# A two-stage codebook convolution on one core: the head of the program reordered

## The chip, the cores and the metric

The kernel runs on one core of one Trainium2 chip. The metric is the device time of one execution in microseconds (us), the median of several runs. Before the change it is 2680.17 us (three runs, 2678.79 to 2683.46). All times in this document are in us unless ns stands there.

The core has five instruction streams that run side by side and wait for each other by semaphores: PE (TensorE, matrix products; its weight loads are shown as PEld), DVE (VectorE), ACT (ScalarE), POOL (GpSimd) and SP (SyncE, which here only issues transfers). Transfers (DMA) are issued by SP and, for some, by POOL, and run on 16 DMA engines. Matrix products read from the on-chip memory SBUF and write into PSUM, which has eight banks.

## The reference, cut to what matters

For each of 16 images (256 channels, 28 x 28) the reference normalizes the channels in groups of 8, runs two "convolutions by codebook", and adds gates and residuals:

```python
def amm_conv3x3(x, centroids, w_sub, stride=1):
    patches = jax.lax.conv_general_dilated_patches(x, (3, 3), (stride, stride), 'SAME')
    p = patches.reshape(B, C, s, Ho * Wo).transpose(0, 3, 1, 2)
    d = jnp.sum(p * p, axis=-1)[..., None] - 2.0 * jnp.einsum('bncs,cks->bnck', p, centroids) + ...
    attn = jax.nn.softmax(-d, axis=-1)
    lut = jnp.einsum('cks,cso->cko', centroids, w_sub)
    out = jnp.einsum('bnck,cko->bno', attn, lut)
...
out = amm_conv3x3(x, centroids1, wsub1); out = relu(bn(out))
out = amm_conv3x3(out, centroids2, wsub2); out = se_layer(bn(out))
return x + relu(out + x)          # the x of the inner sum is the normalized one
```

For each channel and pixel the nine taps of the 3 x 3 patch are compared with 16 centroids, a softmax over the 16 gives weights, and the weighted centroids go through a 9 x 256 matrix per channel.

## The kernel before, in words

**Blocks.** The kernel works in fp32. An image is cut into four blocks: two halves of the channels (`hh`) times two halves of the rows (`t`, 14 rows, 392 pixels). 16 images and two layers make 128 blocks, numbered j; block j begins in step g = 2j, and its work is spread over some four steps. What block j does:

- `patches` (L363) loads two tiles `pt` of 64 channels each, `p` = 0 and 1, from the padded image in DRAM (`home1` in layer 1, `home2` in layer 2). Each tile takes six transfers: for each row dy of the 3 x 3 window one of 16 x 8 runs (L368, the taps of columns 0 and 1) and one of 8 x 8 runs (L372, column 2). A tap s of a channel lies in partition `tap_row(s)` of the channel's 16 (L60); partitions that hold no tap hold 1.0 from a clearing at the start, and one of them, `BIAS_ROW`, carries a bias. There are two `pt` buffers in all, so a tile can be loaded only when the logits that read it one block earlier are done.
- `logits` (L377), four calls `mm` = 0 to 3, two for each tile: 16 small products each into two double banks of PSUM (32 records of PE each, because an fp32 product takes two passes). `exps` (L392) on ACT turns them into exponentials.
- `num_b` (L442), "nb" on PE: the sums over the 16 centroids and the numerator of tap 8. `split_r` and `join_r` (L456, L460) put the sums into `r`; `split_q` and `join_q` (L466, L471) put tap 8 into `qo`. The splits are on ACT, the joins on DVE, and both pairs read the same bank.
- `recip_dve` (L475) inverts `r` on DVE, and `spread` (L484) copies it to the rows of each tap by shuffles.
- `num_a` (L429), "na" on PE, four calls: the numerators of taps 0 to 7, scaled by `scale_a` on DVE (L506) or, for one of them, by `copy_a` on ACT and `scale_q` on POOL (L497). The results, `q`, stay in SBUF.
- `product` (L514), "acc" on PE: the 128 x 128 products with the sub-weights. The four blocks of an image are combined in seven products instead of eight (a Strassen scheme), with differences of `q` made on POOL (`mix`, L523) and sums and differences of sub-weights (`combine`, L202). Their order is in `PRODUCTS` (L43): the first, A11, uses block 0's `q`; the second, S1, uses the difference of blocks 1 and 0.

**The order is written out by hand.** `at(step, sub, function, ...)` puts a call into a table, and the table is run through in order of (step, sub) (L1101). Each engine carries out its instructions in exactly this order, and so does SP's queue of transfers. PSUM is dealt out in the same way: four double banks, and a role (`ROLES`, L47) minus half the step, modulo 4, says which (L111); `small_bank` (L278) is the same for small products.

**The head of the program.** Before the table starts, block 0's way is cleared by hand: the first image is loaded by halves, its statistics (`gn_stats`, `gn_mean`, `gn_var`, L308 to L343: DVE, two small products on PE with `gmat`, four small operations on POOL) give mean and scale, `gn_apply` (L348) normalizes on ACT into the padded tile `xpads`, and `to_home1` (L357) writes it to DRAM in two shifted copies. `norm0` (L1078) bundles this for half an image. Around it stand memsets of the `pt` tiles (L1087, L1091 on DVE, L1092 on POOL), and `center_wd` (L1084) which centres the centroids: squares on DVE, a product "sqp" on PE (L288), additions and a mean on DVE. The centring of the second half of the channels is put behind block 0's first logits, at (0, 1.95).

The second image is prepared beside block 0 and 1 (L993 to L1001): `load_x` at (2, 1.65), `gn_stats` at (3, 1.9), `gn_mean` at (3, 2.1), `gn_var` at (4, 2.1), `gn_apply` and `to_home1` at (5, 1.9) and (5, 1.92). For later images the same calls stand in other places of the table and are not touched. Sub-weights of layer 1 are loaded by `load_w` (L189) at steps 1, 3 and 6 as 128 x 9 runs of 512 bytes each.

Of the kernel before, what the change touches and what calls it, by code (L numbers as in the profile page):

```python
# [17 lines left out]
P = 128  # L18
# [39 lines left out]


def tap_row(s):  # L60
    dy, dx = divmod(s, 3)
    return dy + (0, 8, 3)[dx]

# [10 lines left out]
def kernel(  # L74
# [28 lines left out]
    p_ring = ctx.enter_context(tc.tile_pool(name="p_ring", bufs=1, space=PSUM))  # L103

    gmat = const.tile([P, P], F32, name="gmat")
    make_block_diagonal(nc, gmat, 8)
# [12 lines left out]
    def bank(name, step=None, role=None):  # L119
        return banks(name, step, role)[:, 0, :]  # L120

    def after(u, n):
        return None if u["step"] is None else u["step"] + n

    def view(t, off, dims):
        return bass.AP(t.tensor, t.offset + off, [list(d) for d in dims])
# [62 lines left out]
    def load_w(l, n, eng=None):  # L189
        hh, o = SLOTS[n]  # L190
        t = wl[n]
        eng = eng or nc.sync
        if l == 0:
            eng.dma_start(t, ws1[:, NS * hh : NS * hh + NS, o * P : (o + 1) * P])
        else:
            eng.dma_start(t[:, 0:8, :], view(d_wa, hh * 8 * P * C + o * P, [[C, P], [P * C, 8], [1, P]]))
            eng.dma_start(t[:, 8, :], d_wb[hh * P : hh * P + P, o * P : (o + 1) * P])
# [49 lines left out]
    mhalf = const.tile([P, NB], F32, name="mhalf")  # L247
    one = const.tile([P, 1], F32, name="one")
    nc.gpsimd.memset(one, 1.0)
    nc.gpsimd.memset(mhalf, -0.5)  # L250
# [27 lines left out]
    def small_bank(name, step):  # L278
        return bank(name, step, step and ROLES["small"][step % 2])

# [82 lines left out]
    def patches(u, p, single=None):  # L363
        hm = (home1 if u["l"] == 0 else home2)[u["b"]]
        at0 = ((u["hh"] * P + 8 * 8 * p) * 2) * HROW + RT * u["t"] * PW
        pt = u["pt", p]
        for dy in range(3):
            nc.sync.dma_start(  # L368
                pt[dy::8, :, : PTW - 2],
                view(hm, at0 + dy * PW, [[HROW, 16], [16 * HROW, 8], [1, PTW - 2]]),  # L370
            )
            (single or nc.sync).dma_start(  # L372
                pt[3 + dy :: 16, :, : PTW - 2],
                view(hm, at0 + dy * PW + 2, [[2 * HROW, 8], [16 * HROW, 8], [1, PTW - 2]]),
            )

    def logits(u, mm):  # L377
        bs = []
        for i in range(4):
            if i % 2 == 0:  # L380
                bs.append(banks("lg", after(u, mm // 2), ROLES["lg", mm][i // 2]))
            bk = bs[-1][:, i % 2, :]
            for c in range(4):
                nc.tensor.matmul(  # L384
                    bk[32 * c : 32 * c + 32, :N].rearrange("p (r w) -> p r w", w=W),
                    lhsT=wts["wd", u["hh"]][32 * i : 32 * i + 32, mm, c, :],
                    rhs=u["pt", mm // 2][32 * i : 32 * i + 32, 4 * (mm % 2) + c, :].rearrange("p (r w) -> p r w", w=PW)[:, :, :W],
                    start=True, stop=True,
                )
        u["lg", mm] = bs  # L390
# [523 lines left out]
    for j, u in enumerate(blocks):  # L914
# [22 lines left out]
        at(g + 2, 1.25, recip_dve, u)  # L937
        at(g + 2, 1.3, split_q, u)
        at(g + 2, 1.35, join_q, u)
        for i, mm in enumerate(SLOT_MM):  # L940
# [10 lines left out]
    for l in range(2):  # L951
        for b in range(B):
# [3 lines left out]
            for c, w, r, ks in PRODUCTS:  # L956
                step = g + c - (c == 5 and n == 0)
                at(step, 2.0, product, (n, c), us[r], w, ks, step=step)
            for mm in (1, 2, 3, 4, 0):
# [4 lines left out]
            c11, c12, c21, c22 = (0, 0), (0, 1), (1, 0), (1, 1)  # L964
            at(g + 6 - (n == 0), 0.0, acc_copy, l, b, c11, (n, 5))
            at(g + 6, 2.02, acc_copy, l, b, None, (n, 6))
# [17 lines left out]
            if l == 0:  # L984
# [8 lines left out]
                if b + 1 < B:  # L993
                    at(*((g - 2, 2.6) if b else (2, 1.65)), load_x, b + 1)
                    for q in range(NB):
                        at(*((g, 0.3) if b else (3, 1.9)), gn_stats, b + 1, q)
                    at(g + 3 - 2 * (b > 0), 2.1, gn_mean, b + 1, step=g + 3 - 2 * (b > 0))
                    at(g + 4 - (b > 0), 2.1, gn_var, b + 1, step=g + 4 - (b > 0))
                    for q in range(NB):
                        at(g + 5 - (b > 0), 1.9, gn_apply, b + 1, q)  # L1000
                        at(g + 5 - (b > 0), 1.92, to_home1, b + 1, q)  # L1001
            else:
# [19 lines left out]

    at(1, 1.65, load_w, 0, "A11")
    at(3, 1.65, load_w, 0, "S3")
# [61 lines left out]

    nc.vector.memset(pts[0][:, :4], 1.0)  # L1087
    norm0(0)
    for i in range(2):
        to_home1(0, 0, i)  # L1090
    nc.vector.memset(pts[0][:, 4:], 1.0)  # L1091
    nc.gpsimd.memset(pts[1], 1.0)  # L1092
    center_wd(0)
    norm0(1)
    at(0, 1.95, center_wd, 1)
    at(-0.5, 0.7, to_home1, 0, 1)
# [87 lines left out]
def _lay_out(inputs):  # L1184
# [45 lines left out]
    arrays["in_cwb1"] = cwb.reshape(P, -1)  # L1230
    arrays["in_ws1"] = ws
    cent, wsub = f(_NAMES[0] + "2"), f(_NAMES[1] + "2")
# [29 lines left out]
```

## Time and profile before

| what | value |
|---|---|
| median of 3 runs | 2680.17 |
| the profiled execution's own time | 2684.49 |
| its span (first to last instruction) | 2683.0 |
| mean granted clock of PE | 0.993 |
| PE busy | 2613.8 (97%) |
| DVE, ACT, POOL busy | 1773.8, 1354.7, 1903.7 |
| bytes moved, mean rate | 374.39 MB, 140 GB/s |
| first logits of block 0 start | 26.19 |
| first logits of block 4 (second image) start | 103.33 |

The profile was taken in one execution by the hardware profiler. In its rows an operation stands with its line of the kernel, what it writes and reads (`lg<-pt,wd` is the logits from patches and centroids), the shape, and the number of instructions; in the order of time a row has the start, the length and, in brackets, how long the engine was idle before it and what ended that wait. "issue" means that the profile shows no wait. The starts of PE's matrix products are recorded, their ends are modelled. The granted clock is the share of full speed that PE's throttle let through. SPq rows are transfers as they are issued, not as they land. Lines of the profile are quoted in the parts below where they are used.

### The profile page before, as it was taken

The numbers are of one execution on the slowest core, as the hardware profiler recorded it, in microseconds if no ns is written. First come the engines' busy times: TensorE is split into PE (matmuls) and PEld (weight loads), VectorE is DVE, ScalarE is ACT, GpSimd is POOL, SyncE is SP. The second block draws the span as 40 slices with busy tenths as digits, with TensorE's granted clock in tenths as the row PEclk, the third lists the DMA queues.
The fourth block names the chain that finished last, engine by engine and source line by source line (L and its number), as shares of the span: only waits on it lengthen the run. The fifth ranks groups of instructions, "written<-read, shape, count | busy, mean of one in ns | idle before, by whom it ended". The sixth has DMA issues, their size and how long they took to land.

```text
span 2683.0 us, 85705 instructions
## 1 busy us (share of the span) xinstructions
PE 2613.8 (97%) x36984; PEld 1261.1 (47%) x36984; DVE 1773.8 (66%) x3786; ACT 1354.7 (50%) x1873; POOL 1903.7 (71%) x1334
## 2 busy tenths in 40 slices
PE   4999999999999999999999999999999999999997
PEld 1344444444444444444444444444444444444444
DVE  4785666667666556656577767677767677767675
ACT  2443444444445444444455555555555655555653
POOL 3755677666776666766578687788787788787786
PEclk8999999999999999999999999999999999999999
DMA  8665667755666666666584555545555555555551
GB/s 180 162 158 147 155 159 201 195 139 138 158 165 168 178 156 145 164 176 158 127 191 108 111 127 123 116 111 109 122 127 123 116 113 108 121 127 123 116 114 51
DMA packets 223337, 374.39 MB, mean 140 GB/s; under 512 B 30360, under 2 KB 193736, under 8 KB 222952
## 3 DMA queue, kind: packets, MB, share of 16 engines
q1 hardware_dynamic: 216008, 334.87, 54.0%
q0 software_dynamic: 6944, 33.95, 3.5%
q8 instruction: 295, 4.83, 0.8%
q14 instruction: 90, 0.74, 0.1%
HBM read 288.93 MB, written 79.80 MB: 137 GB/s over the span
## 4 chain that ended last, share of the span: by engine, by line
PE 86%; DMA 1%; POOL 1%; issue 1%; DVE 1%; ACT 0%; SPq 0%; POOLq 0%; DVEq 0%; ACTq 0%
PE acc L518 46%; PE lg L384 15%; PE na L434 12%; PE nb L448 12%; DMA home<-hpad,col 1%; POOL qp L527 1%; PE sep L814 0%; ACT e L395 0%; DMA pt<-home 0%; PE sep L803 0%; DVE qp L510 0%; DVE rb L491 0%; POOL home L590 0%; POOL qo L525 0%; PE sqp L288 0%
## 5 line engine op out<-in xcount | busy, mean ns | idle before, releaser
L395 ACT ACTIVATE e<-lg 128x784 f32<-128x784 f32 x960 | 738.8, 821 | 720.2 <-PE lg L384 714.9
L527 POOL TENSOR_TENSOR qp<-qp,qp 128x784 f32<-128x784 f32 x512 | 944.6, 1870 | 163.5 <-DVE qp L510 163.0
L518 PE MATMUL acc<-qp,w_S 128*128 128x392 f32 x2048 | 743.2, 503 | 7.7 <-POOL qp L527 6.3
L491 DVE STREAM_SHUFFLE rb<-r 128x392 f32<-128x392 f32 x1024 | 550.6, 604 | 0.0
L518 PE MATMUL acc<-qp,w_A 128*128 128x392 f32 x1536 | 546.5, 499 | 0.1
L518 PEld LDWEIGHTS acc<-qp,w_S 128*128 128x128 f32 x2048 | 376.1, 190 | 356.6 <-POOL qp L527 39.1
L384 PE MATMUL lg<-pt,wd 32*32 32x392 f32 x16384 | 500.6, 504 | 27.0 <-DMA pt<-home 16.3
L518 PEld LDWEIGHTS acc<-qp,w_A 128*128 128x128 f32 x1536 | 284.1, 190 | 247.9 <-DVE qp L510 37.6
L510 DVE TENSOR_TENSOR qp<-na,rb 128x784 f32<-128x784 f32 x352 | 334.1, 972 | 98.1 <-PE na L434 84.9
L462 DVE SCALAR_TENSOR_TENSOR r<-nb,kst,r 128x392 f32<-128x392 f32 x128 | 79.9, 624 | 464.5 <-ACT r L458 464.5
L448 PE MATMUL nb<-e,cwb 64*32 64x392 f32 x8192 | 382.4, 497 | 2.1 <-issue 1.0
L434 PE MATMUL na<-e,cwa 64*32 64x392 f32 x8192 | 377.5, 494 | 0.1
L476 DVE RECIPROCAL r<-r 128x392 f32<-128x392 f32 x128 | 333.2, 2603 | 4.4
L499 POOL TENSOR_TENSOR qp<-qp,rb 128x784 f32<-128x784 f32 x160 | 297.4, 1871 | 2.4
L448 PEld LDWEIGHTS nb<-e,cwb 64*32 64x32 f32 x8192 | 181.4, 107 | 195.8 <-issue 57.1
L384 PEld LDWEIGHTS lg<-pt,wd 32*32 32x32 f32 x16384 | 127.5, 103 | 309.0 <-issue 261.6
L499 POOL TENSOR_TENSOR qo<-qo,rb 128x392 f32<-128x392 f32 x128 | 132.0, 1031 | 197.7 <-DVE rb L487 197.5
L434 PEld LDWEIGHTS na<-e,cwa 64*32 64x32 f32 x8192 | 182.5, 106 | 186.8 <-issue 78.0
L590 POOL DMA_INDIRECT home<-hpad,col x60 | 60.6, 1011 | 185.9 <-DMA home<-hpad,col 91.2
L458 ACT ACTIVATE r<-nb,kst 128x392 f32<-128x392 f32 x128 | 86.8, 678 | 177.4 <-PE nb L448 177.4
L419 POOL TENSOR_TENSOR z<-z,mx 128x1568 f32<-128x1568 f32 x32 | 92.1, 2879 | 86.4 <-DVE mx L413 86.4
L504 ACT COPY qp<-na 128x784 f32<-128x784 f32 x160 | 130.1, 813 | 26.0 <-PE na L434 24.0
(154 smaller groups left out, 1744.5 us busy)
## 6 DMA issues: line engine op xcount, KB each, us to landing
pt<-home SPq DMA_DIRECT2D x768, 209.0 KB
pt<-home SPq DMA_DIRECT2D x756, 104.5 KB
home<-xpad SPq DMA_DIRECT2D x31, 899.0 KB
xt<-in_x SPq DMA_DIRECT2D x30, 784.0 KB
out_dram<-y SPq DMA_DIRECT2D x32, 392.0 KB
w_S<-d_wS SPq DMA_DIRECT2D x4, 576.0 KB
st<-in_wsub SPq DMA_DIRECT2D x4, 512.0 KB
st<-d_wa SPq DMA_DIRECT2D x16, 128.0 KB
```

The source lines that it names most:

```text
L384: nc.tensor.matmul(bk[32 * c : 32 * c + 32, :N].rearrange("p (r w) -> p r w", w=W), lhsT=wts["wd", u["hh"]][32 * i : 32 * i + 32, mm, c, : ...
L395: nc.scalar.activation(eg[:, 2 * i : 2 * i + 2, :], bk[:, :, :N], AF.Exp, scale=2.0)
L419: nc.gpsimd.tensor_tensor(zk, zk, mx.unsqueeze(2).to_broadcast([P, N // 4, K]), ALU.subtract)
L434: nc.tensor.matmul(bs[32 * i : 32 * i + 32, r, :N], lhsT=wts["cwa", u["hh"]][64 * r : 64 * r + 64, mm, i, :], rhs=es[64 * r : 64 * r + 64, ...
L448: nc.tensor.matmul(bs[32 * i : 32 * i + 32, r, :N], lhsT=wts["cwb", u["hh"]][64 * r : 64 * r + 64, mm, i, :], rhs=es[64 * r : 64 * r + 64, ...
L476: nc.vector.reciprocal(u["r"], u["r"])
L491: nc.vector.stream_shuffle(rb[:, r, :], u["r"], mask_of(2 * mm + r))
L499: nc.gpsimd.tensor_tensor(q, q, u.pop(("rb", mm)), ALU.mult)
L504: nc.scalar.copy(pair(u, mm), u.pop(("na", mm))[:, :, :N])
L510: nc.vector.tensor_mul(pair(u, mm), u.pop(("na", mm))[:, :, :N], rb)
L518: nc.tensor.matmul(accs[key][:, :N], lhsT=wl[w][:, k, :], rhs=us["q", k], start=first and n == 0, stop=last and n == len(ks) - 1,)
L527: nc.gpsimd.tensor_tensor(pair(out_u, mm), pair(in0, mm), pair(in1, mm), ALU.subtract)
```

## The change

Eight edits, all in the head of the program except the taps and the form of the sub-weights:

- The clearing of the first `pt` tile moves from two memsets on DVE to one activation on ACT, which copies a column of ones over the tile; that column, `one`, is made ahead of everything else on POOL.
- `center_wd(1)` moves from (0, 1.95) to ahead of the table, so its products on PE stand before block 0's logits.
- Block 0's logits `mm` = 1 go to the double banks of role 2 instead of role 1; the small product of step 4 gets another bank.
- For blocks 0 and 1, `split_q` and `join_q` move ahead of the reciprocal.
- The first image's product A11 and the copy of its result move one step later, from step 4 to 5 and from 5 to 6, as in all other images.
- The second image's load moves from step 2 to 1, its `gn_mean` from (3, 2.1) to (4, 1.02), `gn_var` from (4, 2.1) to (4, 1.11), `gn_apply` and `to_home1` from step 5 to 4. On PE the first small product of the statistics moves from ahead of block 2's first logits to behind block 1's nb; on SP's queue the home write moves from behind block 3's second patches to ahead of them.
- The taps lie in other partitions of the 16: taps of the first window row in 0, 8, 5 (before 0, 8, 3), of the second in 4, 12, 13 (before 1, 9, 4), of the third in 1, 9, 2 (before 2, 10, 5). The patches' transfers have the same sizes and other target rows.
- The sub-weights of layer 1 are laid out so that a transfer reads one run of 4608 bytes per partition.

```diff
+TAPS = ((0, 8, 5), (4, 12, 13), (1, 9, 2))
 def tap_row(s):
-    dy, dx = divmod(s, 3)
-    return dy + (0, 8, 3)[dx]
+    return TAPS[s // 3][s % 3]
...
+    one = const.tile([P, 1], F32, name="one")
+    nc.gpsimd.memset(one, 1.0)
     gmat = const.tile([P, P], F32, name="gmat")
...
         if l == 0:
-            eng.dma_start(t, ws1[:, NS * hh : NS * hh + NS, o * P : (o + 1) * P])
+            eng.dma_start(t.rearrange("p s n -> p (s n)"), ws1[(2 * hh + o) * P : (2 * hh + o + 1) * P, :])
...
-        return bank(name, step, step and ROLES["small"][step % 2])
+        return bank(name, step, step and (1 if step == 4 else ROLES["small"][step % 2]))
...
+        n = PTW - 2
         for dy in range(3):
             nc.sync.dma_start(
-                pt[dy::8, :, : PTW - 2],
-                view(hm, at0 + dy * PW, [[HROW, 16], [16 * HROW, 8], [1, PTW - 2]]),
+                pt[TAPS[dy][0] :: 8, :, :n], view(hm, at0 + dy * PW, [[HROW, 16], [16 * HROW, 8], [1, n]])
             )
             (single or nc.sync).dma_start(
-                pt[3 + dy :: 16, :, : PTW - 2],
-                view(hm, at0 + dy * PW + 2, [[2 * HROW, 8], [16 * HROW, 8], [1, PTW - 2]]),
+                pt[TAPS[dy][2] :: 16, :, :n], view(hm, at0 + dy * PW + 2, [[2 * HROW, 8], [16 * HROW, 8], [1, n]])
             )
...
-                bs.append(banks("lg", after(u, mm // 2), ROLES["lg", mm][i // 2]))
+                role = ROLES["lg", mm if u["step"] or mm != 1 else 2][i // 2]
+                bs.append(banks("lg", after(u, mm // 2), role))
...
-        at(g + 2, 1.3, split_q, u)
-        at(g + 2, 1.35, join_q, u)
+        at(g + 2, 1.3 if j > 1 else 1.06, split_q, u)
+        at(g + 2, 1.35 if j > 1 else 1.21, join_q, u)
...
-                step = g + c - (c == 5 and n == 0)
-                at(step, 2.0, product, (n, c), us[r], w, ks, step=step)
+                at(g + c, 2.0, product, (n, c), us[r], w, ks, step=g + c)
...
-            at(g + 6 - (n == 0), 0.0, acc_copy, l, b, c11, (n, 5))
+            at(g + 6, 0.0, acc_copy, l, b, c11, (n, 5))
...
-                    at(*((g - 2, 2.6) if b else (2, 1.65)), load_x, b + 1)
+                    at(*((g - 2, 2.6) if b else (1, 1.65)), load_x, b + 1)
...
-                    at(g + 3 - 2 * (b > 0), 2.1, gn_mean, b + 1, step=g + 3 - 2 * (b > 0))
-                    at(g + 4 - (b > 0), 2.1, gn_var, b + 1, step=g + 4 - (b > 0))
+                    at(*((g + 1, 2.1) if b else (4, 1.02)), gn_mean, b + 1, step=g + 1 if b else 4)
+                    at(*((g + 3, 2.1) if b else (4, 1.11)), gn_var, b + 1, step=g + 3 if b else 4)
                     for q in range(NB):
-                        at(g + 5 - (b > 0), 1.9, gn_apply, b + 1, q)
-                        at(g + 5 - (b > 0), 1.92, to_home1, b + 1, q)
+                        at(g + 4, 1.9, gn_apply, b + 1, q)
+                        at(g + 4, 1.92, to_home1, b + 1, q)
...
-    at(1, 1.65, load_w, 0, "A11")
+    at(1, 1.66, load_w, 0, "A11")
...
-    nc.vector.memset(pts[0][:, :4], 1.0)
+    nc.scalar.activation(pts[0].rearrange("p s n -> p (s n)"), one.to_broadcast([P, 8 * PTW]), AF.Copy)
     norm0(0)
     for i in range(2):
         to_home1(0, 0, i)
-    nc.vector.memset(pts[0][:, 4:], 1.0)
     nc.gpsimd.memset(pts[1], 1.0)
     center_wd(0)
     norm0(1)
-    at(0, 1.95, center_wd, 1)
+    center_wd(1)
...
-    arrays["in_ws1"] = ws
+    arrays["in_ws1"] = ws.reshape(P, 2, NS, 2, ch // 2).transpose(1, 3, 0, 2, 4).reshape(4 * P, -1)
```

Two memset instructions on DVE fall away and one activation on ACT comes in; otherwise every engine has the same instructions, some in another order.

More of the change, by code (lines that the diff above doesn't have):

```diff
@@ L247 @@
     mhalf = const.tile([P, NB], F32, name="mhalf")
-    one = const.tile([P, 1], F32, name="one")
-    nc.gpsimd.memset(one, 1.0)
     nc.gpsimd.memset(mhalf, -0.5)
```

## The prediction

> **What bounds the kernel now.** I read the page first, then a table by stretches of 20 us, then the order of time engine by engine over the first 130 us.
>
> ```profile
> PE 2613.8 (97%) x36984; PEld 1261.1 (47%) x36984; DVE 1773.8 (66%) x3786; ACT 1354.7 (50%) x1873; POOL 1903.7 (71%) x1334
> PE 86%; DMA 1%; POOL 1%; issue 1%; DVE 1%; ACT 0%; SPq 0%; POOLq 0%; DVEq 0%; ACTq 0%
> ```
> ```profile
> 20.00:40.00 20.00, 9.24 (x140) 3.34 (x146) 3.59 (x13) 7.19 (x9) 8.74 (x16) 0.98 0.96 190
> 40.00:60.00 20.00, 14.47 (x256) 4.56 (x256) 11.27 (x26) 8.21 (x11) 2.66 (x5) 0.68 0.71 149
> 60.00:80.00 20.00, 17.48 (x278) 7.70 (x278) 12.12 (x32) 7.10 (x10) 3.39 (x6) 0.91 0.75 156
> 80.00:100.00 20.00, 16.95 (x274) 6.62 (x274) 13.65 (x31) 11.44 (x16) 16.29 (x11) 1.00 0.88 248
> 100.00:120.00 20.00, 16.67 (x258) 7.18 (x274) 13.88 (x30) 7.04 (x10) 20.00 (x12) 0.91 0.65 140
> 120.00:140.00 20.00, 19.68 (x262) 9.75 (x238) 16.59 (x42) 6.94 (x10) 15.65 (x11) 1.00 0.45 102
> ```
> The page says that TensorE (PE) is busy 97% of the span and carries 86% of the chain that ended last. The table (the first number after the stretch is its length, then PE, weight loads, DVE, ACT, POOL, granted clock, DMA share, GB/s) shows where the rest is: PE works 9 to 17 of each 20 us before 120 us, partly at a low clock, and nearly all of them after. From there on PE is never waiting for long, so whatever the head of the program gains comes out at the end one for one, and nothing else in this change can. The question is when the eighth step starts: the first block of the second image, whose logits begin at 103.33.
>
> ```profile
> 26.19 4.09 PE L384 MATMUL lg<-pt,wd 32*32 32x392 f32 x64 [8.04 <-DMA pt<-home]
> 30.25 1.22 PE L288 MATMUL sqp<-sq,nhalf_sb 128*128 128x256 f32 x2
> 32.42 1.19 PE L288 MATMUL sqp<-sq,nhalf_sb 128*128 128x256 f32 x2 [0.94 <-DVE sq L283]
> 33.54 2.77 PE L384 MATMUL lg<-pt,wd 32*32 32x392 f32 x64
> 39.94 1.62 PE L384 MATMUL lg<-pt,wd 32*32 32x392 f32 x32 [3.63 <-DMA pt<-home]
> 41.49 5.02 PE L448 MATMUL nb<-e,cwb 64*32 64x392 f32 x64
> 51.16 1.62 PE L384 MATMUL lg<-pt,wd 32*32 32x392 f32 x32 [3.71 <-issue]
> 52.71 4.54 PE L434 MATMUL na<-e,cwa 64*32 64x392 f32 x64
> 62.51 0.36 PE L322 MATMUL gnp<-gn_mv,gmat 128*128 128x4 f32 x2 [4.33 <-DVE gn_mv L317]
> 64.40 3.80 PE L448 MATMUL nb<-e,cwb 64*32 64x392 f32 x64
> 69.09 4.22 PE L518 MATMUL acc<-qp,w_A 128*128 128x392 f32 x12
> 80.42 1.45 PE L384 MATMUL lg<-pt,wd 32*32 32x392 f32 x32 [0.43 <-DVE qp L510]
> 86.81 1.58 PE L518 MATMUL acc<-qp,w_S 128*128 128x392 f32 x4 [1.21 <-POOL qp L527]
> 93.20 0.93 PE L518 MATMUL acc<-qp,w_S 128*128 128x392 f32 x2 [0.54 <-POOL qp L527]
> 103.33 1.64 PE L384 MATMUL lg<-pt,wd 32*32 32x392 f32 x32 [3.76 <-DMA pt<-home]
> 104.90 4.03 PE L448 MATMUL nb<-e,cwb 64*32 64x392 f32 x64
> 116.80 2.92 PE L434 MATMUL na<-e,cwa 64*32 64x392 f32 x64
> 119.65 0.94 PE L384 MATMUL lg<-pt,wd 32*32 32x392 f32 x32
> ```
> These are PE's rows (start, length, what; in brackets the idle time before and what ended it). Idle gaps of 3.63, 3.71, 4.33 and 3.76 us stand there, and behind each the same work is slow: 32 logits take 1.62 instead of 0.94, a sum (nb, na) 3.80 to 5.02 instead of 2.92. The granted clock (0.68 in 40 to 60) says why. So a gap costs itself and about 2 us more.
>
> **The change part by part.**
>
> ```profile
> 7.69 2.10 POOL L256 TENSOR_SCALAR rs_t<-gn_var 128x1 f32<-128x1 f32 x1 [2.48 <-DVE nrm L340]
> 7.97 1.46 DVE L1091 MEMSET pt<- 128x1680 f32 x1 [0.30 <-issue]
> 11.10 1.05 ACT L349 ACTIVATE xpad<-xt,nrm 128x784 f32<-128x784 f32 x1 [8.78 <-POOL nrm L343]
> 16.39 0.57 SPq L368 DMA_DIRECT2D pt<-home  x1
> 18.43 0.40 POOL L256 TENSOR_SCALAR rs_t<-gn_var 128x1 f32<-128x1 f32 x1 [4.53 <-DVE nrm L340]
> ```
> 1. *Clearing on ACT.* One column of additions on POOL took 2.10 us while DVE's memset ran beside it, and 0.40 later without one. It stands on the way to the first normalization (11.10), the home write and the patches (16.39). Without the memset: 1.7 us sooner, first logits at 24.5. The new clearing on ACT has no row; scaled from 784 columns in 1.05 us, 3360 take 4.5 at most, from about 2.3; ACT is idle until then (8.78 us), so I take nothing, with 2.5 us left before it would count. The memset of `one` ahead of everything else is a single column: nothing.
>
> 2. *Centring and other banks.* The two sqp products leave PE's row between the two halves of block 0's logits and go to 17 to 21 us, where PE only waits. The first half then costs 2 x 1.62, to 27.8 (before 30.28: the old one also waited inside for a bank). The second half waits for ACT's four exponentials (821 ns each, below) and ends near 31 instead of 36.3.
>
> 3. *The next patches.* They may start when the first half is done and took 39.94 - 30.28 = 9.66 us. Kept at that, block 1 starts at 37.4 (-2.5). The second tile is freed 5 us sooner and isn't waited for. PE is idle for 6 us here and cold behind it, as before.
>
> ```profile
> 50.53 0.53 DVE L473 SCALAR_TENSOR_TENSOR qo<-nb,kst,qo 128x392 f32<-128x392 f32 x1
> 56.70 1.86 DVE L510 TENSOR_TENSOR qp<-na,rb 128x784 f32<-128x784 f32 x2 [1.35 <-PE na L434]
> 81.53 1.98 ACT L349 ACTIVATE xpad<-xt,nrm 128x784 f32<-128x784 f32 x2
> 92.42 0.59 SPq L368 DMA_DIRECT2D pt<-home  x1
> ```
> ```profile
> L395 ACT ACTIVATE e<-lg 128x784 f32<-128x784 f32 x960 | 738.8, 821 | 720.2 <-PE lg L384 714.9
> L491 DVE STREAM_SHUFFLE rb<-r 128x392 f32<-128x392 f32 x1024 | 550.6, 604 | 0.0
> L476 DVE RECIPROCAL r<-r 128x392 f32<-128x392 f32 x128 | 333.2, 2603 | 4.4
> ```
> 4. *Early joins.* The gap ahead of 51.16 is called "issue", but the bank that those logits need is freed by the join of qo, which ends at 51.06, behind the reciprocal. From the end of nb (46.51) that is 4.55 us; without the 2.60 of the reciprocal 1.95. nb now ends at 37.4 + 6.6 = 44.0, the logits run at 46.1 (-5.1), and after a gap of 1 us at full clock. The reciprocal itself starts 0.5 later: it ends at 48.6, six shuffles (550.6/1024 = 0.54 apart) at 51.9, three scalings at 54.8, where the old ones ended at 58.56. PE, done with na at 50, waits about 3 us for the first of them.
>
> 5. *Second image's norm out of the way.* The product at 62.51 made block 2 wait for statistics that wait for the image. Now it stands behind nb; block 2 starts with the third scaling, at 54.9 (before 62.85: -8.0). Its nb ends at 58.7. The price: DVE's join of block 1 stands behind the statistics' two small products; I charge 1.2 us. Joins, 2.60, 3.2 and 2.9 put the last scaling at 70.9, against the 80.4 that the row at 80.42 waits for.
>
> 6. *Product A11 one step later.* It filled PE from 69.09 while DVE made block 1's factors; 18 matmuls at 4.22/12 are 6.3 us. That cover is gone: PE waits some 2 us before and 2 us after na, and A11 runs from 69.9 to 76.2. Block 3 starts there (80.42: -4.2). But the differences on POOL, which held the S1 product from 86.81 to 94.13, now start 9.5 us sooner and are ready: 16 matmuls end at 86.3 (-7.8).
>
> 7. *Home sooner.* The normalization at 81.53 moves to about 63, and its home write with it; on SP's queue it now stands ahead of block 3's second patches, which aren't free to load before 70, so it holds nothing up. The patches that were issued at 92.42, behind that write, can go when their tile is free, at 81. PE reaches block 4 after 0.94 + 2.92 + 0.94 + 0.93 at 92.0; 10.9 us for the load (92.42 to 103.33, with the write beside it) are just enough. So 11.3 sooner, and not cold: 1.64 - 0.94 + 4.03 - 2.92 = 1.8 more.
>
> 8. *Sub-weights in one run, taps in other rows.* Four loads that nobody waits for: nothing. The taps have no row; I take the load times as they are. All patch loads change, so both ends are kept below.
>
> The sum: 13.1 us. The profiled execution took 2684.49 (span 2683.0), which gives 2671.4; against the median of 2680.17, 4.3 lower, **2667**.
>
> **The rivals.**
>
> *Faster patches* (2662). Two loads set the pace: the first (9.8 us) and block 1's (9.66). In 20 to 40, mostly patches, a DMA share of 0.96 moved 190 GB/s; in 80 to 100, with home writes, 0.88 moved 248. If the new rows bring the patches to 248 x 0.96/0.88 = 270, a load shortens by up to 30%, 2.9 us; counted in full on the first and for 2 on the second, where ACT's exponentials come next, that is 5. Against it: the 16 engines take the same rows in the same order. [...]
>
> *Cold gaps, late patches* (2672). The gaps of 3 us that I leave ahead of the scalings lie just under the 3.63 that made PE slow. Two cold stretches cost 2 x 2.3; so does one late load at block 4 (3 us and 1.8). [...]
>
> *Given back* (2679). The head moves about 190 GB/s on average; squeezed by 11 us it needs 210. If SP's transfers are the limit throughout, each wait returns as a wait for patches and only steps 1 and 2 are left, or less.
>
> *Slower* (2800).
> ```profile
> 130.82 0.99 PE L384 MATMUL lg<-pt,wd 32*32 32x392 f32 x32
> 148.70 0.94 PE L384 MATMUL lg<-pt,wd 32*32 32x392 f32 x32
> ```
> One tile is freed at 131.8 and needed at 148.7: 16.9 us for a load of some 9.7. If the new rows made a load 1.75 times as long, every block would wait; each us beyond costs 124 blocks 1 us each, +124 - 13. Nothing speaks for it but that all 1,524 loads change.
>
> **How the numbers follow.** Forecast 0.42 (2664 to 2670), faster patches 0.18, cold or late 0.22, given back 0.10, slower 0.08. The range 2660 to 2677 takes in the first three. A measurement tells 0.2%, 5.4 us, from no change: faster 0.82, same 0.10, slower 0.08.
>
> **What would show it.** First addition on POOL near 0.4 us, first logits near 24.5; block 1's near 37; no wait of 4 us at the second image's product; logits of block 2 near 55; a gap of 2 to 3 us ahead of A11, near 70; block 4 near 92 without a DMA wait and nb there at 2.9. If block 4 starts before 90, the taps did it; if nb rows show 3.8 to 5 after 55, the clock did not hold; if waits on patches appear after 130, the rows are worse.

## The result and the profile after

The changed kernel takes **2665.2 us** (median of 4 runs, 2659.66 to 2669.58) where before takes 2679.57 (4 runs): a ratio of 0.9947, 95% interval 0.9932 to 0.9961, or 14 us less. Timed again in the second series below it was 0.9953 (0.9936 to 0.9970; 2662.58 against 2673.95). The forecast was 2667, with 2660 to 2677 as its range. The number held; what it is made of did not quite, as the runs below show.

The page of the kernel after, in the profiled execution (2669.58 us): busy times, the hardware queue's row (packets, MB, share of the 16 DMA engines' time), and the chain that ended last.

```profile
PE 2602.3 (98%) x36984; PEld 1261.0 (47%) x36984; DVE 1773.3 (66%) x3784; ACT 1356.5 (51%) x1874; POOL 1901.2 (71%) x1334
...
q1 hardware_dynamic: 211912, 334.87, 51.3%
...
PE 83%; POOL 3%; DMA 3%; issue 1%; ACT 1%; DVE 1%; POOLq 0%; DVEq 0%; ACTq 0%
```

The 20 us stretches of the kernel after from 40 us on, as they were shown of before (length, PE, weight loads, DVE, ACT, POOL, granted clock, DMA share, GB/s):

```profile
40.00:60.00 20.00, 15.33 (x288) 4.92 (x280) 13.21 (x31) 9.36 (x13) 4.55 (x5) 0.85 0.65 150
60.00:80.00 20.00, 16.16 (x278) 7.01 (x270) 12.94 (x32) 9.57 (x14) 7.78 (x8) 0.98 0.95 263
80.00:100.00 20.00, 18.97 (x343) 8.07 (x340) 15.23 (x33) 9.50 (x15) 15.61 (x11) 1.00 0.73 194
100.00:120.00 20.00, 18.56 (x230) 9.19 (x200) 18.24 (x29) 7.96 (x11) 19.74 (x12) 1.00 0.44 103
120.00:140.00 20.00, 17.73 (x247) 7.98 (x248) 14.68 (x40) 6.80 (x11) 10.80 (x8) 0.91 0.23 54
```

PE is busier where it was meant to be, in 40 to 60 and in 80 to 120. The last row is new: PE was busy 19.68 of these 20 us before and is busy 17.73 now, with the clock at 0.91. Something stands in PE's way behind 120 us that did not stand there before.

PE's rows in order of time, kernel after (an "nb" behind the first logits of block j+1 is block j's; x32 are two records for each of 16 products, and more of how an fp32 product is carried out the rows don't show):

```profile
24.00 3.31 PE L386 MATMUL lg<-pt,wd 32*32 32x392 f32 x64 [3.51 <-issue]
28.59 3.35 PE L386 MATMUL lg<-pt,wd 32*32 32x392 f32 x64 [1.28 <-DMA pt<-home]
38.06 1.62 PE L386 MATMUL lg<-pt,wd 32*32 32x392 f32 x32 [6.13 <-DMA pt<-home]
47.20 0.95 PE L386 MATMUL lg<-pt,wd 32*32 32x392 f32 x32 [1.84 <-ACT e L397]
53.54 1.49 PE L386 MATMUL lg<-pt,wd 32*32 32x392 f32 x32 [2.56 <-DVE qp L512]
55.30 2.16 PE L386 MATMUL lg<-pt,wd 32*32 32x392 f32 x32 [0.27 <-DVE qp L512]
57.39 4.44 PE L450 MATMUL nb<-e,cwb 64*32 64x392 f32 x64
72.13 4.22 PE L520 MATMUL acc<-qp,w_A 128*128 128x392 f32 x12
78.25 0.94 PE L386 MATMUL lg<-pt,wd 32*32 32x392 f32 x32
93.76 1.36 PE L386 MATMUL lg<-pt,wd 32*32 32x392 f32 x21
96.95 2.86 PE L450 MATMUL nb<-e,cwb 64*32 64x392 f32 x64
122.27 4.43 PE L450 MATMUL nb<-e,cwb 64*32 64x392 f32 x64 [3.71 <-DVE gn_dv L330]
```

Block 1 begins at 38.06 (39.94 before), block 2 at 55.30 (62.85), A11 at 72.13, block 3 at 78.25 (80.42), block 4 at 93.76 (103.33). Block 4 waits for no transfer, and its nb runs at full clock (2.86 where it was 4.03; granted clock 1.00 in 80 to 100). Then the last row: 3.71 us of idleness, ended by a small DVE operation of the third image's group mean (gn_dv), and 4.43 us for an nb that takes 2.9 elsewhere.

What held that small operation up, in the order of time of DVE and POOL, kernel after:

```profile
113.51 6.33 DVE L613 TENSOR_SCALAR c<-c 128x144 f32<-128x144 f32 x1
...
117.87 1.87 POOL L501 TENSOR_TENSOR qp<-qp,rb 128x784 f32<-128x784 f32 x1
```

L613 is one line of `code_spread`, a preparation of layer 2's codebook, placed by hand at (9 + 2o, 1.9); it only negates 144 columns. It took 6.33 us and ended at 119.84, when POOL's last operation of a chain without a pause (from 97.88 to 119.74) had ended. The group mean of the third image stands behind it on DVE. PE's small product for that mean stands ahead of the nb and lies in the same bank that the nb is to write (role 1 at step 9 and role 2 at step 10 both give double bank 1), so PE waits until DVE has read it.

### The profile page after: what moved, and what is told of

Its sections match the earlier page's. It is cut to its first block, busy times and chain, and to the rows that moved or that the text cites. A ratio compares the mean times of both kernels' runs of the same rounds, so it can differ in the third digit from the quotient of the medians.

```text
span 2668.1 us, 85705 instructions
## 1 busy us (share of the span) xinstructions
PE 2602.3 (98%) x36984; PEld 1261.0 (47%) x36984; DVE 1773.3 (66%) x3784; ACT 1356.5 (51%) x1874; POOL 1901.2 (71%) x1334
## 4 chain that ended last, share of the span: by engine, by line
PE 83%; POOL 3%; DMA 3%; issue 1%; ACT 1%; DVE 1%; POOLq 0%; DVEq 0%; ACTq 0%
PE acc L520 44%; PE lg L386 15%; PE na L436 12%; PE nb L450 12%; DMA home<-hpad,col 3%; POOL qp L529 2%; POOL qo L527 0%; POOL home L592 0%; ACT e L397 0%; PE sep L816 0%; PE sep L805 0%; DVE qp L512 0%; DVE rb L493 0%; ACT hpad L571 0%; ACT qo L470 0%
## 5 line engine op out<-in xcount | busy, mean ns | idle before, releaser
L450 PEld LDWEIGHTS nb<-e,cwb 64*32 64x32 f32 x8192 | 181.5, 108 | 194.3 <-issue 50.9
```

Of the source, the lines that this page charges most:

```text
L450: nc.tensor.matmul(bs[32 * i : 32 * i + 32, r, :N], lhsT=wts["cwb", u["hh"]][64 * r : 64 * r + 64, mm, i, :], rhs=es[64 * r : 64 * r + 64, ...
```

## The experiments

Ratios are to the kernel before, timed side by side on the same chip, in three series. Its median was 2673.14 in the first (new and old tap rows, A11 back, `code_spread` later), 2673.95 in the second (after again, late joins, late norm, both edits) and 2672.71 in the third (before again, clearing alone, dummy matmuls, third order of rows). So a time that an expectation gives beside the 2679.6 of the result is compared by its ratio. Medians of different series are compared with care, and differences under 4 us are within their intervals.

### The kernel before and after, again

Before, unaltered:

> The kernel before again, unaltered, for a second profile: the first (span 2683.0) was longer than the middle of its later runs, 2673. If the lead that the changed kernel's traces gain between blocks 5 and 67 (10 to 18 us against the first profile of before) is mostly that one execution's own slowness, this profile is near 2673 and ahead of the first by 5 to 11 us at block 67, with fewer sums of 3.2 to 3.9 us in the first layer. If the lead belongs to the change, this profile runs like the first one there, within 3 us.

Measured: 0.9995 (0.9983 to 1.0007), a profile of 2675.31 us, ahead of the first one by 9 us at the end. So 9 us of the lead that one reads off the two first profiles are that one execution of before, not the change. From here on this second profile is the one to compare with.

After, unaltered:

> The changed kernel again, unaltered, timed beside the others. If the tap rows (0.9973 alone) and the order of the first stages (0.9974 without them) are two separate gains, the changed kernel has both: 0.9947 of before, as first measured, near 2659 where before is 2673, and patch transfers at 51.3% of the 16 engines as in its first profile. If the one stands in the place of the other, it lies with e2_old_taps: 0.997, 2665 to 2667.

Measured: 0.9953, q1 at 50.9%, a profile of 2664.72 us. Its rows on PE:

```profile
52.21 0.95 PE L386 MATMUL lg<-pt,wd 32*32 32x392 f32 x32 [2.56 <-DVE qp L512]
...
54.96 2.86 PE L450 MATMUL nb<-e,cwb 64*32 64x392 f32 x64
...
61.83 1.62 PE L386 MATMUL lg<-pt,wd 32*32 32x392 f32 x32 [2.38 <-DMA pt<-home]
...
93.01 2.86 PE L450 MATMUL nb<-e,cwb 64*32 64x392 f32 x64
...
118.83 5.05 PE L450 MATMUL nb<-e,cwb 64*32 64x392 f32 x64 [4.20 <-DVE gn_dv L330]
```

The same 2.56 us of idleness that was followed by slow logits (1.49) and a slow nb (4.44) in the first profile is followed by fast ones here (0.95, 2.86). The stall ahead of block 4's nb (122.27 and 118.83) is in both.

Start times of three nb on PE, read from the rows in time order, and the lead over before's second profile:

| kernel | nb of block 3 | nb of block 5 | nb of block 124 | lead at 3, 5, 124 |
|---|---|---|---|---|
| before, second profile | 103.71 | 148.65 | 2564.32 | |
| after, first profile | 96.95 | 145.40 | 2558.72 | 6.8, 3.3, 5.6 |
| after, second profile | 93.01 | 142.57 | 2553.90 | 10.7, 6.1, 10.4 |
| tap rows alone | 104.35 | 148.67 | 2557.76 | -0.6, 0.0, 6.6 |
| after with the old tap rows | 93.56 | 142.51 | 2556.13 | 10.2, 6.1, 8.2 |
| after with the third order of rows | 92.02 | 136.61 | 2542.83 | 11.7, 12.0, 21.5 |

Each line is one execution, and the last column wanders by some 5 us from one to the next: the six times of the third order lie between 2653.65 and 2664.34. What stands out is the drop between the first two numbers (given back at the stall) and the gain between the last two. The drop is larger than the starts show, because block 3's nb is slow in before:

```profile
103.71 4.69 PE L448 MATMUL nb<-e,cwb 64*32 64x392 f32 x64
```

Behind this nb, where the next logits start, before stands at 108.33 and after's second profile at 95.80, a lead of 12.5 us, of which 6.1 are left at block 5. The 6.4 us lost are the wait of 4.20 and the 2.2 that the nb behind it takes longer (5.05 against 2.86). The large lead of the third order comes in part from a shorter stall (1.42 us), not from its rows.

### The tap rows

In the kernel before, the new rows alone (the two transfers in `patches` write to `TAPS[dy][0] :: 8` and `TAPS[dy][2] :: 16`, as in the change):

```diff
+TAPS = ((0, 8, 5), (4, 12, 13), (1, 9, 2))
...
-    dy, dx = divmod(s, 3)
-    return dy + (0, 8, 3)[dx]
+    return TAPS[s // 3][s % 3]
```

> The kernel before, with nothing changed but the partitions on which the nine taps of a patch tile lie (and so the rows that the patch loads write). Theory (the gain is the order of the first stages; the taps are neutral): the time of before, 2679.6 us within 0.2%, block 4 near 103. Rival A (the new rows load faster, and the 7 us of lead that the changed kernel gained between 130 and 1400 us of the first layer are theirs): 2671 to 2673, block 1's first logits 1 to 3 us sooner than 39.94, fewer short waits in the first layer. Rival B (those 7 us are a difference between one execution and another): 2679.6, but a spread between runs as wide as the changed kernel's, 10 us.

Measured: 0.9973 (0.9958 to 0.9988), 2666.97: rival A by the time, but not by its sign in the head. Block 1's first logits come at 39.34, 0.6 us sooner than 39.94 and not 1 to 3; the head is where it was, and 6 us come later.

In the kernel after, the old rows:

```diff
-TAPS = ((0, 8, 5), (4, 12, 13), (1, 9, 2))
+TAPS = ((0, 8, 3), (1, 9, 4), (2, 10, 5))
```

> The changed kernel with the taps on the old partitions; everything else of the change stays. Theory (taps neutral): 2665 us, as the changed kernel, with the lead of block 4 near 6 us and of block 67 near 15. Rival A (taps worth 7 us in the first layer): 2672, the lead at block 4 as it was and none gained between 130 and 1400 us. Rival C (the order of the start needs the faster rows: with the old ones block 4 waits for its patches, 1 to 3 us, and is cold behind it): 2668 to 2670, a DMA wait ahead of block 4.

Measured: 0.9974 (0.9965 to 0.9983), 2667.32: rival A again, from the other side. The two gains, each some 0.26%, add up to the change's 0.47 to 0.53%. The hardware queue's row shows where the rows act. Before's second profile, the tap rows alone, after with the old rows:

```profile
q1 hardware_dynamic: 216008, 334.87, 54.2%
```
```profile
q1 hardware_dynamic: 216008, 334.87, 51.2%
```
```profile
q1 hardware_dynamic: 211912, 334.87, 54.5%
```

With the old rows the queue's packets take 54.0 to 54.5% of the engines' time (four profiles), with the new ones 50.9 to 51.4% (nine), for the same bytes. The 4096 packets fewer come from the sub-weights' longer runs; these were not run alone, and with the old rows the share is no lower for them.

In the kernel after, a third order of rows:

```diff
-TAPS = ((0, 8, 5), (4, 12, 13), (1, 9, 2))
+TAPS = ((2, 10, 7), (0, 8, 3), (1, 9, 6))
```

> The changed kernel with a third order of tap rows: (2, 10, 7), (0, 8, 3), (1, 9, 6). Like the old one it puts four of nine taps on rows 0 to 3 of each 16, two on 4 to 7, three on 8 to 11 and none on 12 to 15, where the new one has 3, 2, 2, 2. [...]

Measured: 0.9949 (0.9933 to 0.9964), 2658.04, and on its page:

```profile
q1 hardware_dynamic: 211912, 334.87, 50.7%
```

An order with the old counts (4, 2, 3, 0) does as well as the new one (3, 2, 2, 2): the share of 50.7% lies with the new rows' and not with the old ones', and the ratio with after's 0.9947 and 0.9953 and not with 0.9974. This speaks against the even spread over groups of four rows as the cause. In groups of four rows the six transfers of the third order even reach the same groups as those of the old one, only in another sequence. What the old rows do worse remains open: rows 3, 4, 5 of the third column follow rows 0, 1, 2 of the first in step, but that this is the cause was not tried.

How shorter transfers reach the end time is shown in part. PE's waits between 480 and 1460 us (line waited for, us in total, times, longest), before's second profile and then the tap rows alone:

```profile
PE acc L518 <- POOL qp L527: 3.9, 10, 0.6
PE acc L518 <- DMA pt<-home: 1.1, 2, 0.6
```
```profile
PE acc L519 <- POOL qp L528: 1.5, 5, 0.6
```

Waits for patches themselves are 1.1 us in all; products that wait for POOL's differences make 2.4 more. That is 3.5 of 6 us, in one execution each, and after with the old rows has 4.3 there and its second profile with the new rows 3.3, so the rest is not accounted for.

### The parts of the head

The clearing on ACT alone, with `one` early, in the kernel before:

```diff
+    one = const.tile([P, 1], F32, name="one")
+    nc.gpsimd.memset(one, 1.0)
     gmat = const.tile([P, P], F32, name="gmat")
...
-    nc.vector.memset(pts[0][:, :4], 1.0)
+    nc.scalar.activation(pts[0].rearrange("p s n -> p (s n)"), one.to_broadcast([P, 8 * PTW]), AF.Copy)
-    nc.vector.memset(pts[0][:, 4:], 1.0)
```

> The kernel before with only the start changed: the first patch tile cleared by ACT, the column of ones written first. Prediction's step 1: first logits at 24.5 instead of 26.19, 1.7 us sooner; what comes behind is set by transfers, so 0.5 to 1.7 us of it stay: 0.9994 to 1.0 of before. Rival (nothing stays, block 2 waits for the second image's statistics as in before): 1.0000.

Measured: 0.9989 (0.9979 to 0.9998), 3 us less where 0.5 to 1.7 were expected (the interval holds both), and the first logits at the forecast time:

```profile
24.53 4.09 PE L384 MATMUL lg<-pt,wd 32*32 32x392 f32 x64 [8.12 <-DMA pt<-home]
...
98.54 1.28 PE L384 MATMUL lg<-pt,wd 32*32 32x392 f32 x32 [3.80 <-DMA pt<-home]
```

In before's second profile these two stand at 26.14 and 102.02: the 1.6 us are 3.5 at block 4. They stay, which speaks against the rival; why more than 1.6 came of them, two single executions don't show.

The early joins, undone in the kernel after:

```diff
-        at(g + 2, 1.3 if j > 1 else 1.06, split_q, u)
-        at(g + 2, 1.35 if j > 1 else 1.21, join_q, u)
+        at(g + 2, 1.3, split_q, u)
+        at(g + 2, 1.35, join_q, u)
```

> The changed kernel with the joins of the first two blocks' second half back behind the reciprocal. Prediction's step 4: the bank of block 1's second logits is freed 2.6 us later, so the wait of 1.84 us becomes some 4.4, the logits behind it run at the low clock, block 2 starts 3 to 4 us later, and what is behind takes over about as much: 2 to 5 us slower than the changed kernel. Rival (the head waits for transfers later on, so the loss is absorbed by block 3 or 4): within 1 us of the changed kernel.

Measured: 0.9940 (0.9919 to 0.9961), 2658.84: no slower than the kernel after. The rows are late at first and not at the end:

```profile
47.58 0.95 PE L386 MATMUL lg<-pt,wd 32*32 32x392 f32 x32 [3.71 <-issue]
...
55.72 2.86 PE L450 MATMUL nb<-e,cwb 64*32 64x392 f32 x64
...
119.59 4.56 PE L450 MATMUL nb<-e,cwb 64*32 64x392 f32 x64 [3.13 <-DVE gn_dv L330]
```

The wait of 3.71 is back, but the next nb is only 0.8 us later than in after's second profile (54.96), since the gap of 2.56 behind na is gone: the logits take the bank of the scalings in either case. At the stall the kernels are 0.8 apart, one nb later 0.3. Step 4's rows were right, its gain in time is not there.

The second image's norm, back at before's places:

```diff
-                    at(*((g - 2, 2.6) if b else (1, 1.65)), load_x, b + 1)
+                    at(*((g - 2, 2.6) if b else (2, 1.65)), load_x, b + 1)
...
-                    at(*((g + 1, 2.1) if b else (4, 1.02)), gn_mean, b + 1, step=g + 1 if b else 4)
-                    at(*((g + 3, 2.1) if b else (4, 1.11)), gn_var, b + 1, step=g + 3 if b else 4)
+                    at(g + 3 - 2 * (b > 0), 2.1, gn_mean, b + 1, step=g + 3 - 2 * (b > 0))
+                    at(g + 4 - (b > 0), 2.1, gn_var, b + 1, step=g + 4 - (b > 0))
-                        at(g + 4, 1.9, gn_apply, b + 1, q)
-                        at(g + 4, 1.92, to_home1, b + 1, q)
+                        at(g + 5 - (b > 0), 1.9, gn_apply, b + 1, q)
+                        at(g + 5 - (b > 0), 1.92, to_home1, b + 1, q)
...
-    at(1, 1.66, load_w, 0, "A11")
+    at(1, 1.65, load_w, 0, "A11")
```

> The changed kernel with the second image's load, statistics, normalization and home write back at the places that before gave them. Prediction's steps 5 and 7 (8.0 us at block 2 less what the later steps give back, 11.3 at block 4, of which the start, the joins and A11 are not undone): block 2 waits for the statistics' product again, block 4 for its patches; 5 to 8 us slower than the changed kernel. Rival (given back: the lead at block 4 falls anyway by the stall ahead of 122.27, which goes when the product and POOL's chain move): no slower than 2 us.

Measured: 0.9970 (0.9959 to 0.9982), 2666.19, 3.6 us over the kernel after in the same series, between the two expectations:

```profile
59.85 0.56 PE L324 MATMUL gnp<-gn_mv,gmat 128*128 128x4 f32 x2 [6.78 <-DVE gn_mv L319]
...
75.05 3.04 PE L436 MATMUL na<-e,cwa 64*32 64x392 f32 x48 [3.68 <-DVE gn_var L340]
...
103.03 2.86 PE L450 MATMUL nb<-e,cwb 64*32 64x392 f32 x64
```

With the two waits for statistics block 3's nb comes 10 us later (103.03 against 93.01). Half of that is gone by block 5's (147.93 against 142.57), because here the negation took 0.55 us and the stall is 1.7. So by these two profiles the largest part of the head's gain is this one, and half of it is given back at the stall; the two intervals overlap, so the 3.6 us themselves are not certain. The centring ahead of the table, the other banks and the sub-weights' longer runs were not run alone.

A11 back one step earlier:

```diff
-                at(g + c, 2.0, product, (n, c), us[r], w, ks, step=g + c)
+                step = g + c - (c == 5 and n == 0)
+                at(step, 2.0, product, (n, c), us[r], w, ks, step=step)
...
-            at(g + 6, 0.0, acc_copy, l, b, c11, (n, 5))
+            at(g + 6 - (n == 0), 0.0, acc_copy, l, b, c11, (n, 5))
```

> The changed kernel with product A11 back one step earlier, ahead of block 2's sums na, as before had it. Theory of the prediction (the later place only moves PE's filling; it was costed at nothing apart from the cover lost): A11's 6.1 us fill the waits of 1.55, 0.66 and 1.63 us around na, na runs warm at 2.9 instead of 2 x 1.6, but the last scalings come some 3 us later; block 3 then starts 75.5 to 78 instead of 78.25 and the time is 2662 to 2666. Rival (the later place is needed: with A11 in front, na, its join and all that hangs on it come 4 to 6 us later and block 4 too): 2668 to 2671.

Measured: 0.9935 (0.9919 to 0.9951), 2655.63. Beside a before of 2679.6 the expected 2662 to 2666 are 0.9934 to 0.9949, so this is the fast end of the theory, and the rival (2668 to 2671, 0.9957 to 0.9968) is out.

```profile
61.86 4.22 PE L520 MATMUL acc<-qp,w_A 128*128 128x392 f32 x12 [0.25 <-DVE gn_var L340]
...
79.46 1.58 PE L520 MATMUL acc<-qp,w_S 128*128 128x392 f32 x4 [1.21 <-POOL qp L529]
...
117.30 2.87 PE L450 MATMUL nb<-e,cwb 64*32 64x392 f32 x64 [1.69 <-DVE gn_dv L330]
```

A11 fills PE while DVE works, the S1 product then waits for POOL's differences again, and block 3's nb comes no sooner (94.00). But POOL's operations lie differently against DVE's, the negation took only 0.50 us, and the stall shrinks to 1.69. The later place of A11 is not needed for the gain; whether the earlier one is better as such or by this chance can't be told.

### The stall

In the kernel after, `code_spread` moved behind the group mean:

```diff
-        at(9 + 2 * o, 1.9, code_spread, o)
+        at(9 + 2 * o, 2.12, code_spread, o)
```

> The changed kernel with one helper step of the second layer's weight preparation (the code spread, whose negation on DVE took 6.33 us from 113.51 while POOL worked without a pause) put behind the third image's group mean on DVE instead of ahead of it. Theory (the wait of 3.71 us ahead of the nb at 122.27 is this one DVE instruction standing in front of the mean's four small ones): that wait goes, with the 1.5 us of cold matmuls behind it, about 5 us: 2660, and no nb there longer than 2.9. Rival (POOL's chain itself is late, and PE will wait for POOL or for DVE's next join instead): the wait turns up within two blocks under another name, 2664 to 2666.

Measured: 0.9936 (0.9920 to 0.9953), 2658.01. The nb of block 4 runs without a wait, so `code_spread` is what held it. Part of the wait returns one place later under another name, as the rival had it:

```profile
116.59 2.92 PE L450 MATMUL nb<-e,cwb 64*32 64x392 f32 x64
121.64 0.95 PE L386 MATMUL lg<-pt,wd 32*32 32x392 f32 x32 [2.13 <-DVE hpad L557]
```

Against the second profile of after the lead at block 5's nb grows from 6.1 to 8.3 us. From the logits behind block 3's nb to block 5's nb it is 40.3 us in before's second profile, 46.8 in after's and 42.5 here: 4.3 of the 6.4 us come back. How long the negation takes differs with where it starts in POOL's chain. In the third order of rows it started as one operation of POOL ended (at 108.71) and the next began:

```profile
107.70 1.01 POOL L527 TENSOR_TENSOR qo<-qo,qo 128x392 f32<-128x392 f32 x1
108.58 0.23 DVE L613 TENSOR_SCALAR c<-c 128x144 f32<-128x144 f32 x1
108.68 1.83 POOL L529 TENSOR_TENSOR qp<-qp,qp 128x784 f32<-128x784 f32 x1
```

Started at 108.58 it took 0.23 us; started at 109.56 in after's second profile, inside the operation of POOL that ran from 109.11 to 110.94, it took 6.83 and ended at 116.39, when POOL's chain had ended at 116.29. But how long it takes beside the chain differs: in four profiles (both of after, the old rows, the dummy matmuls) 6.33 to 8.03 us, past operations of POOL of 1.0 to 2.7 us each to the end of the chain, and with the late joins only 1.93. There other operations of `code_spread` were long as well:

```profile
111.40 1.93 DVE L613 TENSOR_SCALAR c<-c 128x144 f32<-128x144 f32 x1
...
114.17 1.69 DVE L618 TENSOR_SCALAR cmean<-cmean 128x9 f32<-128x9 f32 x1
...
117.01 1.76 DVE L620 TENSOR_SCALAR c<-c 128x144 f32<-128x144 f32 x1
```

In after's first profile, behind POOL's chain, L618 and L620 take 0.17 and 0.23 us. PE waited 3.13 us for the late joins' `code_spread`, and still 1.42 in the third order, where L619 took 2.69. So it is the whole of `code_spread` beside POOL's chain that holds the mean, not the negation alone. Its reductions of 144 columns took 0.28 to 0.40 us beside POOL's operations as without them. What makes these DVE operations long beside POOL's, and what decides which of them, is not shown.

Both edits together:

> The changed kernel with both edits that shortened it alone: the code spread behind the group mean (a wait of 3.71 us and 1.5 cold behind it) and product A11 one step earlier (block 2 and 3 sooner by some 3 us, and the stall 1.69 in place of 3.71). If the gains are separate: 2 us less than e4_a11_back, since only 1.69 of the stall was left there, 2653 where before is 2673. If the wait ahead of the nb near 117 in e4_a11_back comes from POOL's chain and not from the code spread: the same as e4_a11_back, 2655 to 2656.

Measured: 0.9938 (0.9919 to 0.9957), 2657.92, not better than either alone. The four variants at 0.9935 to 0.9940 all lie below the kernel after (0.9947 and 0.9953), but every interval overlaps with its own, so that any of them beats it is likely at best and not shown. The nb is free of its wait, but the logits behind it wait 2.88 us for DVE's addition to hpad, which now stands behind the negation.

A11 back, and dummy matmuls in PE's gaps:

```diff
+            if u["step"] == 2 and mm == 0 and i == 0:
+                for _ in range(8):
+                    nc.tensor.matmul(bk[:, :304], lhsT=nhalf_sb, rhs=kst[:, :304], start=True, stop=True)
...
+        if u["step"] == 0 and mm == SLOT_MM[-1]:
+            for _ in range(18):
+                nc.tensor.matmul(bs[:, 1, N:512], lhsT=nhalf_sb, rhs=kst[:, :120], start=True, stop=True)
```

> The changed kernel with product A11 one step earlier, as in e4_a11_back, and dummy matmuls (their results are not used) in PE's two early gaps, 8 ahead of block 1's first logits and 18 small ones behind block 0's sums na, so that the clock stays up. If the cold stretches behind the gaps of 5.5 and 2.57 us cost what their rows say (1.62 less 0.94 and 4.36 less 2.9 behind the first, 4.16 less 1.9 and 4.09 less 2.9 behind the second): nb of block 1 starts 3 to 4 us sooner than 56.02 and the time is 1 to 4 us under e4_a11_back's 2655.6. Rival (POOL's differences, for which PE waits 1.21, 0.22, 0.23 and 0.54 us from 79 on, set the pace by then): the lead is gone at block 4, and the time is within 1 us of e4_a11_back.

Measured: 0.9948 (0.9932 to 0.9964), 2659.82, not faster than without them.

```profile
36.87 0.95 PE L389 MATMUL lg<-pt,wd 32*32 32x392 f32 x32 [1.25 <-DMA pt<-home]
37.75 2.90 PE L456 MATMUL nb<-e,cwb 64*32 64x392 f32 x64
...
44.27 4.70 PE L439 MATMUL na<-e,cwa 64*32 64x392 f32 x64
...
119.27 4.80 PE L456 MATMUL nb<-e,cwb 64*32 64x392 f32 x64 [5.24 <-DVE gn_dv L330]
```

The first slow stretch is cured (0.95 and 2.90 for 1.62 and 4.36), and a new one appears at once in na, behind only 1.84 us of idleness, with a granted clock of 0.59 from 44 to 48 us. So block 1's nb starts at 55.85, 0.2 us sooner and not the 3 to 4 expected. Block 3's nb is 1.9 us sooner (92.09 against 94.00), and then the negation, started at 108.81, takes 8.03 us and PE waits 5.24. This is the stall at its plainest: 2 us won in the head, 3.5 more of waiting lost behind it.

## Why the prediction was right, and where it was not

**Steps 1 to 3** held within a us: POOL's first addition took 0.41, the first logits came at 24.00 (forecast 24.5), the first half ended at 27.3 (27.8), the second at 31.9 (31), block 1 came at 38.06 and 37.59 (37.4). Block 0's second half waited 1.28 us for its tile, where step 2 had ACT's exponentials end that wait. ACT's clearing took 3.00 us and delayed nothing.

**Steps 4 to 7** held as rows: block 1's second logits at 47.20 and 45.87 (46.1), A11 at 72.13 and 68.70 (69.9), block 3 at 78.25 and 74.82 (76.2), block 4 without a DMA wait at 93.76 and 90.32 (92.0). Against the profile from which it was worked, block 3's nb was to start at 92.9 and starts at 93.01 in after's second profile. The two profiles lie on the two sides of each number, from A11 on because behind the gap of 2.56 us PE's granted clock was low in one (0.73 in 52 to 56 us, 0.50 in 56 to 60) and not in the other (1.00 in both). Its price, from these logits to the end of the nb, is 8.29 us against 5.61 (53.54 to 61.83, 52.21 to 57.82), 2.7 us; the rival had 2.3. That PE always stays fast behind gaps of up to 3 us, as the sum takes it, no run shows: behind 2.54 to 2.57 us it was slow in four profiles of seven. The later place of A11 turned out not to be needed, and the early joins by themselves brought nothing. One wait is missing from the forecast: in after's second profile, where PE came sooner, block 2's second half waits 2.38 us for its patches (61.83), with slow work behind it (logits 1.62, na 3.78).

**The sentence that failed** is the one behind the sum: that from 120 us on whatever the head gains comes out one for one, and nothing else in this change can. Both halves are wrong. Behind block 3's nb, where the 13.1 us were forecast, the lead was 12.5 (13.1 over before's first profile), and at block 5 it was 6.1: 6.4 are given back at a wait that I did not expect, because before has nearly nothing of it; before's negation stands later against PE (2.94 us at 122.64), and its nb waits 0.32 us at most. The rival called given back had the right sign and in the main the wrong carrier: not SP's transfers but `code_spread` on DVE beside POOL's chain. And **step 8** costed the tap rows at nothing where they bring 0.27% alone (0.12 to 0.42%). The rival for them was placed in the head, where the runs show none of it: with the new rows alone block 3's nb stands 0.6 us later (104.35 against 103.71), not sooner.

So 13.1 forecast for the head became about 6 behind the stall (without the new rows the change brings 5.8 us, 2667.32 against 2673.14), the taps added about 6, and the sum came out at 11 to 14. The total was right because two errors of like size had opposite signs; in that the number was lucky.

## What to carry to other kernels

When the order of a head is tightened, look at what every engine does at the first place where the gained time meets the steady state: here helper operations on DVE that had had room now stand inside POOL's unbroken chain, and half of the gain is lost there. Before reading small leads off two profiles, take a second profile of the same kernel; one execution of before was 9 us from another. And a change in the layout of all transfers deserves its own run, even where no wait names them.

## What the runs showed of the hardware

Behind a gap of 2.54 to 2.57 us on PE the same work was slow or not: of seven profiles that have it ahead of block 1's last logits, four show slow work behind it (32 logits in 1.49 or 1.60 us, or 64 in 4.16) and three do not (32 in 0.95). The granted clock in 52 to 56 us, behind it, was 1.00 in after's second profile and 0.50 with A11 earlier.

```profile
52.00:56.00 4.00, 2.98 (x93) 1.11 (x101) 4.00 (x11) 2.58 (x4) 1.41 (x2) 1.00 0.27 72
```
```profile
52.00:56.00 4.00, 3.86 (x64) 0.67 (x64) 4.00 (x10) 2.19 (x3) 1.64 (x2) 0.50 0.20 54
```

Behind a gap of 1.84 us it was so too: na, behind the logits that end the gap, took 2.90 us in after's second profile and 4.70 with the dummy matmuls, at granted clocks of 1.00 and 0.59 in 44 to 48 us. A 144-column negation on DVE took from 0.23 to 8.03 us by when it met POOL's chain, while reductions of the same 144 columns beside that chain took 0.28 to 0.40. The order of the nine tap rows changed the time that the transfers' packets took by 6% (54.2% of 2673.8 us against 51.2% of 2667.5), for the same bytes, sizes and packet count.
